# One place in the issue order for every step of a graph-network kernel

## The chip, the cores and the metric

The kernel runs on one core of a Trainium2 chip. It has four compute engines with a queue of their own each: TensorE (PE in the profile, with its weight loads as PEld), VectorE (DVE), ScalarE (ACT) and GpSimd (POOL). SyncE (SP) issues most transfers. Each queue is worked off in the order in which the program issued into it, and an instruction waits by semaphore for what other engines or transfers make. The metric is device time in microseconds, the median of several runs.

## The reference

128 graphs of 64 nodes with 128 features. For every pair of nodes (i, j) of a graph a small network computes a message, the messages of the neighbours are summed, and a second network updates the node:

```python
pair_feats = concatenate([f_i, f_j])               # (128, 64, 64, 256)
messages = _mlp(pair_feats, msg weights) * coupling_matrix[..., None]
agg = sum(messages, axis=2)
updated = part_feats + _mlp(concatenate([part_feats, agg]), upd weights)

def _mlp(x, ...):
    h = layernorm(relu(x @ w0 + b0), g0, be0)
    h = layernorm(relu(h @ w1 + b1), g1, be1)
    return h @ w2 + b2
```

The adjacency is sparse (about one pair in eight, with the diagonal), so the kernel computes messages for existing edges only.

## The kernel before

Each graph gets a list of 640 edge slots, in five tiles of 128. Two graphs are a pair `p` (64 pairs), two pairs a group `q` of 20 tiles (32 groups), four pairs a block `b` (16 blocks). The edge work is done in chunks `n` of four tiles, 512 edges; there are 160 chunks, five to a group.

**Finding the edges, by pair.** `rank`, `count`, `place` and `place_out` number a block's edges. `distance` (ScalarE, L876) and `make_tp` (VectorE, L882) make a 0/1 table of which node owns each slot. `marks` (TensorE, L908) and `compare` (VectorE, L916) make the same for the other node of each edge. `node_rows` and `stack` (transfers on SyncE, L898) lay both tables into the tile `s`. `node_marks` (a transposing transfer, L1018) makes the table for the sums.

**Layer 0, by chunk.** `rows` multiplies the node features by the two halves of w0; `rows_hi` and `rows_lo` split the product into two parts, `abh` and `abl`. `gather` (L933) multiplies them by `s` into the single PSUM bank `hps`, which gives the layer's sums for 512 edges at once. A chunk spans one, two or more stretches of tables that belong to different graphs; each such piece takes two matmuls, for `abl` and `abh`. `relu0` (ScalarE, L938) empties the bank into `h`. `turn_h` (L943) transposes `h` into the single bank `hT`, and VectorE takes `stats0` of it (L629). After a group's five chunks `root_of` makes the standard deviations on ScalarE.

**Layer 1, by chunk.** `layer1` (L986) runs into one of two banks `z`. The bias enters either by `seed` (ScalarE writes it into the bank ahead) or by `seed_all` on GpSimd (L973) with the ReLU on VectorE (L613). `relu1` and `stats1` follow. After a group, `var1_step` (L646, L647, GpSimd; VectorE for the last group), `root1_of` (L653, ScalarE) and `inverse_of` (L658, VectorE) make the factor of the second normalisation. `weights` (L1029, GpSimd) puts it on the table of `node_marks`, and `reduce_block` (L1044) sums the messages of a block's nodes on TensorE.

**Update, by block.** `sums_out`, `turn`, `turn_out`, `layer_a`, `layer_b`, `layer_c`, `layer_out`, `layer_stats`, `upd_*`, `residual`, `bias0` and `finish` run the second network and write the block out.

**The order.** Nothing is scheduled by the framework. The kernel makes a list `plan` of 4,676 steps, each a call of one of these functions, sorts it and calls them one after the other. A step's key is 144 times a chunk number plus an offset from the table `WHEN`. From chunk 14 to 137 the table has one offset for each remainder of the chunk number by ten, so the order repeats every ten chunks (one block); the start and the end have offsets of their own:

```python
def at(n, tag, fn, *args):
    v = args[0] if args else 0
    v = v.b if isinstance(v, Unit) else v
    t = WHEN.get(f"{fn.__name__}{tag}", {}).get(n % 10 if 14 <= n < 138 else 100 + v, 0)
    plan.append((SCALE * n + t, len(plan), fn, args))
```

At the start `keep_busy` (L1336) issues matmuls whose result nobody reads; 18 instructions in seven steps.

Of the kernel before, what the change touches and what calls it, by code (L numbers as in the profile page):

```python
# [25 lines left out]
    "<lambda>.3": {100: 398},  # L26
    "<lambda>.4": {100: 795},
    "<lambda>.6": {100: 4632},
    "<lambda>.7": {100: 284},
    "ahead.0": {100: 233},  # L30
    "ahead.1": {100: 132},
    "ahead.10": {100: 11},
    "ahead.11": {100: -1},
    "ahead.2": {100: 50},
    "ahead.5": {100: 113},
    "ahead.8": {100: 157},
    "ahead.9": {100: 215},
    "bias0": {3: -1471, 112: -1906, 113: -1642, 114: -17},
    "bias0_0": {115: 1153},
    "bias0_2": {115: 525},  # L40
    "bounds": {100: -15375},
# [8 lines left out]
    "count": {8: -190, 101: 140, 102: 122, 115: -186},  # L50
    "count.0": {100: 47},
    "count_out": {9: -228, 101: -2, 102: 190, 115: -239},
    "count_out.0": {100: 63},
    "degrees": {9: -358, 101: -137, 102: 105, 115: -608},
    "degrees.0": {100: -699},
    "distance": {0: -539, 3: 150, 5: -495, 8: -349, 103: 84, 104: 283, 105: -140, 106: 202,
        107: -511, 108: 189, 158: -852, 159: -528, 160: -749, 161: -525, 162: -737, 163: -1005},
    "distance.0": {100: 181},
    "distance.1": {101: 189},
    "distance.2": {102: 311},  # L60
    "empties.0": {100: 111},
    "empties.1": {100: 152},
    "empties.10": {100: 200},
    "empties.11": {100: 169},
    "empties.2": {100: -14},
    "empties.3": {100: 100},
    "empties.4": {100: 111},
    "empties.5": {100: 55},
    "empties.6": {100: -50},
    "empties.7": {100: -92},  # L70
    "empties.8": {100: -22},
    "empties.9": {100: 128},
    "finish": {8: 220, 110: 217, 111: 771, 112: 335, 113: -14, 114: 4865},
    "finish_0": {115: 6154},
    "finish_2": {115: 6519},
    "flag_in": {100: 118},
    "flag_max": {100: 160},
    "flag_out": {100: 377},
    "flag_sum": {100: 514},
    "flag_turn": {100: 45},  # L80
# [26 lines left out]
    "inverse_of": {0: -228, 5: 130, 125: -359, 126: -111, 127: 59, 128: 506, 129: 147, 130: 64,  # L107
# [44 lines left out]
    "layer_out.uh": {7: -98, 112: 370, 113: 251, 114: 103},  # L152
    "layer_out.uy": {2: 270, 111: -27, 112: 407, 113: 290, 114: 1108},
# [222 lines left out]
def tile_gnn(  # L376
# [293 lines left out]
    def edge_path(es):  # L670
# [257 lines left out]
        def gather(n, j, k):  # L928

            if n not in HP:  # L930
                HP[n] = ps_h.tile([P, CH * P], F32, name="hps")
# [727 lines left out]
```

## Time and profile before

| | us |
|---|---|
| median of 3 runs | 498.48 |
| lowest and highest run | 497.48, 499.75 |
| span of the profiled execution | 497.9 |
| TensorE busy (share of the span) | 486.0 (98%) |
| VectorE busy | 465.2 (93%) |
| ScalarE busy | 397.3 (80%) |
| GpSimd busy | 348.4 (70%) |

The span runs from the first to the last instruction of the profiled execution; for that execution no other time is given. A busy time counts stretches in which at least one instruction of the engine is under way. Matmuls overlap and their ends are modelled, so a busy TensorE need not be one at its peak. In a group's row, the numbers after the bar are the busy time in us, the mean duration of one in ns, the idle time of the engine just before them in us, and what ended most of it.

### The profile page before, as it was taken

The numbers are of one execution on the slowest core, as the hardware profiler recorded it, in microseconds if no ns is written. First come the engines' busy times: TensorE is split into PE (matmuls) and PEld (weight loads), VectorE is DVE, ScalarE is ACT, GpSimd is POOL, SyncE is SP. The second block draws the span as 40 slices with busy tenths as digits, with TensorE's granted clock in tenths as the row PEclk, the third lists the DMA queues.
The fourth block names the chain that finished last, engine by engine and source line by source line (L and its number), as shares of the span: only waits on it lengthen the run. The fifth ranks groups of instructions, "written<-read, shape, count | busy, mean of one in ns | idle before, by whom it ended". The sixth has DMA issues, their size and how long they took to land. (4 is left out here: it accounts for less than half of the span.)

```text
span 497.9 us, 15949 instructions
## 1 busy us (share of the span) xinstructions
PE 486.0 (98%) x5947; PEld 461.3 (93%) x5947; DVE 465.2 (93%) x1225; ACT 397.3 (80%) x907; POOL 348.4 (70%) x563
## 2 busy tenths in 40 slices
PE   7999999999999999999999999999999999999995
PEld 5889999999999999999899999999999999999994
DVE  7999999999999999999999999999999988989985
ACT  6999978878787887878778786888878778867754
POOL 3285776967959676795867859676696859565770
PEclk9999999999999999999999999999999999999998
DMA  4766836367574656854465574656655448625331
GB/s 122 148 145 157 182 99 150 93 167 152 126 140 110 126 142 150 168 122 118 117 143 143 126 153 103 132 128 158 152 123 128 101 112 165 152 74 129 66 34 47
DMA packets 91474, 63.55 MB, mean 128 GB/s; under 512 B 57473, under 2 KB 75522, under 8 KB 91394
## 3 DMA queue, kind: packets, MB, share of 16 engines
q1 hardware_dynamic: 91106, 62.36, 55.9%
q8 instruction: 49, 0.80, 0.7%
q14 instruction: 31, 0.25, 0.2%
q10 hardware_dynamic: 288, 0.13, 0.1%
HBM read 7.15 MB, written 4.19 MB: 23 GB/s over the span
## 5 line engine op out<-in xcount | busy, mean ns | idle before, releaser
L986 PE MATMUL z<-w1c,h 128*128 128x128 f32 x1280 | 190.0, 275 | 0.0
L986 PEld LDWEIGHTS z<-w1c,h 128*128 128x128 f32 x1280 | 172.4, 192 | 4.0 <-DVE uy_st L629 0.2
L938 ACT ACTIVATE h<-hps,b0c 128x512 f32<-128x512 f32 x160 | 109.0, 682 | 36.0 <-PE hps L933 35.5
L629 DVE BATCH_NORM_STATS2 st<-hT 128x6 f32<-128x256 f32 x320 | 122.9, 417 | 7.1 <-PE hT L943 4.8
L629 DVE BATCH_NORM_STATS2 st<-y 128x6 f32<-128x256 f32 x320 | 127.1, 419 | 0.5 <-ACT y L997 0.3
L980 ACT ACTIVATE z<-b1b,m_sd 128x128 f32<-128x128 f32 x320 | 117.3, 368 | 9.2 <-DVE y L613 3.6
L943 PE MATMUL hT<-ident,h 128*128 128x128 f32 x640 | 112.9, 276 | 0.3 <-DVE st L629 0.2
L933 PE MATMUL hps<-s,abl 128*128 128x512 f32 (+3 forms) x256 | 96.6, 380 | 2.6 <-ACT h L938 2.1
L933 PE MATMUL hps<-s,abh 128*128 128x512 f32 (+3 forms) x256 | 89.8, 358 | 0.0
L973 POOL TENSOR_TENSOR u<-b1b,m_sd 128x512 f32<-128x512 f32 x80 | 83.7, 1049 | 7.6 <-ACT m_sd L637 7.6
L943 PEld LDWEIGHTS hT<-ident,h 128*128 128x128 f32 x640 | 76.3, 141 | 3.4 <-issue 1.2
L1029 POOL TENSOR_TENSOR w<-oh,m_q 128x192 f32<-128x192 f16 x126 | 62.1, 514 | 9.4 <-DVE m_q L658 3.1
L916 DVE TENSOR_TENSOR j<-mk,cmpt 128x320 fp32r<-128x320 f32 x124 | 59.4, 479 | 6.3 <-PE mk L908 3.9
L891 POOL CAST i<-tp 128x640 fp32r<-128x640 f16 x58 | 41.8, 720 | 29.3 <-DMA s<-i 27.7
L997 ACT ACTIVATE y<-z 128x512 f32<-128x512 f32 x80 | 47.4, 595 | 17.8 <-PE z L986 17.5
L613 DVE CUSTOM_DVE_ANT_0 y<-z,u 128x512 f32<-128x512 f32 x80 | 54.1, 676 | 4.0 <-PE z L986 3.7
L933 PEld LDWEIGHTS hps<-s,abl 128*128 128x128 f32 x256 | 48.8, 191 | 8.0 <-ACT h L938 3.7
L876 ACT ACTIVATE d<-slot,mid 128x640 f16<-128x640 f16 x64 | 52.1, 818 | 1.7 <-POOL mid L765 1.0
L647 POOL TENSOR_TENSOR m_v<-m_v,st 128x20 f32<-128x20 f32 x31 | 7.3, 234 | 60.9 <-DVE st L629 59.6
L933 PEld LDWEIGHTS hps<-s,abh 128*128 128x128 f32 x256 | 49.1, 192 | 0.2
L1044 PE MATMUL ys<-y,w 128*32 128x128 f32 x1488 | 44.1, 274 | 0.0
L1044 PEld LDWEIGHTS ys<-y,w 128*32 128x32 f32 x1488 | 39.6, 110 | 2.5 <-issue 2.1
(193 smaller groups left out, 887.9 us busy)
## 6 DMA issues: line engine op xcount, KB each, us to landing
s<-i SPq DMA_DIRECT2D x124, 160.0 KB, 3.0
s<-j SPq DMA_DIRECT2D x124, 160.0 KB, 2.8
xn<-in_x_dram SPq DMA_DIRECT2D x15, 256.0 KB, 3.9
out_dram<-uo SPq DMA_DIRECT2D x15, 256.0 KB, 2.5
an<-in_adj_dram SPq DMA_DIRECT2D x16, 128.0 KB, 3.5
oh<-tp SPq DMA_TRANSPOSE x64, 3.0
xn<-in_x_dram SPq DMA_DIRECT2D x2, 128.0 KB, 3.0
out_dram<-uo SPq DMA_DIRECT2D x2, 128.0 KB, 3.4
```

What stands on the lines that cost most here:

```text
L613: nc.vector._custom_dve(TENSOR_ADD_SAT, out=o, in0=ps, in1=sb, s0=BIG, s1=0.0)
L629: nc.vector.bn_stats(st, src.rearrange("p t c -> p c t"))
L876: nc.scalar.activation(D[p], slot.rearrange("p (t e) -> p t e", e=P), AF.Abs, bias=blocks[b]["mid"][:, q:q + 1], scale=-1.0)
L916: nc.vector.tensor_tensor(JR[p][:, c], MK.pop((p, k))[:, 0:HC], cmpt[:, c], op=ALU.is_equal)
L933: nc.tensor.matmul(HP[n][:, c:c + w], lhsT=blocks[g // (2 * PB)]["ab", g // 4 % 2][k][:, g % 4, :], rhs=S[g // 2][:, g % 2, e:e + w], star ...
L938: nc.scalar.activation(H[n], HP.pop(n), AF.Relu, bias=b0c)
L943: nc.tensor.transpose(HT[n][:, t, :], H[n][:, t * P:(t + 1) * P], ident)
L973: nc.gpsimd.tensor_tensor(U[n], bc(W["b1b"], CH), SR[q][:, k:k + CH].unsqueeze(2).to_broadcast([P, CH, C]), op=ALU.mult)
L980: nc.scalar.activation(z_of(n)[:, t, :], W["b1b"], AF.Copy, scale=SR[q][:, k:k + 1])
L986: nc.tensor.matmul(ps[:, t, :], lhsT=H[n][:, t * P:(t + 1) * P], rhs=W["w1c"], start=by_vector(n) and t == 0, stop=True, skip_group_check= ...
L1029: (nc.vector if p == NP - 2 else nc.gpsimd).tensor_tensor(WT[p][:, g], oh, qs, op=ALU.mult)
L1044: nc.tensor.matmul(YS[b][g * N + m * HN:g * N + (m + 1) * HN, k, :], lhsT=w[:, g, m, u, :], rhs=y, start=(u == 0), stop=(u == TH - 1), til ...
```

## The change

The table holds, for every kind of step, one place for each time that the step is put on the list, from 1 to 4,676, each used once. The key is that place alone; chunk number and period no longer enter. Four functions change beside it. `gather` counts the matmuls that a chunk still has to get: the first to be issued, whichever piece it is, has `start`, the last has `stop`, and the others accumulate; before, each piece had a `start` and a `stop` of its own. `upd_shift`, `marks_here` and `rows_here` make their tile in whichever of their steps comes first.

```diff
 WHEN = {
-    "keep_busy.n2": {102: -390},
-    "root1_of": {0: -276, 5: 96, 125: -363, 126: -204, 127: -15, 128: 436, 129: 138, 130: 40,
-        131: 200},
...
+    "keep_busy.n2": (11,),
+    "root1_of": (
+        464, 572, 738, 834, 963, 1131, 1228, 1415, 1533, 1657, 1781, 1955, 2169, 2300, 2439, 2570,
+        2699, 2854, 2989, 3101, 3319, 3396, 3575, 3695, 3842, 3925, 4136, 4259, 4398, 4474, 4557,
+        4603),
...
+        seen = {}
+
         def at(n, tag, fn, *args):
-            v = args[0] if args else 0
-            v = v.b if isinstance(v, Unit) else v
-            t = WHEN.get(f"{fn.__name__}{tag}", {}).get(n % 10 if 14 <= n < 138 else 100 + v, 0)
-            plan.append((SCALE * n + t, len(plan), fn, args))
+            base = f"{fn.__name__}{tag}"
+            k = seen[base] = seen.get(base, -1) + 1
+            t = WHEN[base][k] if base in WHEN else SCALE * n
+            plan.append((t, len(plan), fn, args))
...
         def gather(n, j, k):
-            if n not in HP:
+            start = n not in HP
+            if start:
                 HP[n] = ps_h.tile([P, CH * P], F32, name="hps")
+                LEFT[n] = 2 * len(list(pieces(n)))
+            LEFT[n] -= 1
             g, e, c, w = sorted(pieces(n), key=lambda v: -v[3])[j]
             nc.tensor.matmul(HP[n][:, c:c + w], lhsT=blocks[g // (2 * PB)]["ab", g // 4 % 2][k][:, g % 4, :],
-                             rhs=S[g // 2][:, g % 2, e:e + w], start=(k == 0), stop=(k == 1))
+                             rhs=S[g // 2][:, g % 2, e:e + w], start=start, stop=LEFT[n] == 0,
+                             skip_group_check=True)
...
         def upd_shift(u, q0, q1):
-            if q0 == 0:
-                u.usdb = wide("usdb", u)
+            u.usdb = wide("usdb", u)
...
         def marks_here(p):
-            S[p] = sp.tile([P, 2, CAP], F32R, name="s")
+            if p not in S:
+                S[p] = sp.tile([P, 2, CAP], F32R, name="s")
...
         def rows_here(p, g):
+            if p not in S:
+                S[p] = sp.tile([P, 2, CAP], F32R, name="s")
             nc.scalar.copy(S[p][0:N, g, :], TP[p][g * N:(g + 1) * N])
```

Some places before and after, counted in the sorted list of 4,676 steps:

| step | place before | place after |
|---|---|---|
| `turn_x`, first block, first half | 11 | 1 |
| the three first `keep_busy` | 4, 5, 6 | 11, 24, 26 |
| `relu0` of chunk 0 | 46 | 41 |
| `layer1` of chunk 0 | 168 | 158 |
| last `reduce` | 4,617 | 4,618 |

More of the change, by code (lines that the diff above doesn't have):

```diff
@@ L25 @@
 WHEN = {
[L26 to L41, printed above, removed]
[8 rows of a table removed]
@@ L50 @@
[L50 to L80, printed above, removed]
[26 rows of a table removed]
-    "inverse_of": {0: -228, 5: 130, 125: -359, 126: -111, 127: 59, 128: 506, 129: 147, 130: 64,
[44 rows of a table removed]
-    "layer_out.uh": {7: -98, 112: 370, 113: 251, 114: 103},
-    "layer_out.uy": {2: 270, 111: -27, 112: 407, 113: 290, 114: 1108},
[12 rows of a table removed]
-    "load_adj": {1: -693, 102: -349, 103: -1531},
-    "load_x": {8: -290, 102: 631, 115: 184},
-    "make_tp": {1: -374, 4: 131, 6: -444, 9: -342, 103: 108, 104: 179, 105: 120, 106: 96, 107: -74,
[10 rows of a table removed]
@@ L179 @@
-    "node_marks": {0: -545, 4: 10, 5: 367, 9: -143, 100: -798, 101: 174, 152: 17, 153: 333,
-        154: 534, 155: -146, 156: 563, 157: 63, 158: 368, 159: 445, 160: 688, 161: 506, 162: -255,
-        163: -43},
-    "node_rows": {0: -314, 2: 91, 5: 223, 7: -155, 102: 278, 103: 417, 104: 90, 105: 101, 106: 65,
-        107: -131, 158: -226, 159: 2, 160: -311, 161: 40, 162: 463, 163: 314},
-    "odd_weights": {3: -24, 101: -1531, 102: -1295, 115: -539},
-    "odd_weights.0": {100: -1392},
-    "ones": {100: 12389},
@@ L187 @@
-    "place": {1: -331, 101: 214, 102: -38, 115: -472},
-    "place_first": {100: 127},
-    "place_out": {3: 174, 101: 237, 102: -124, 115: -233},
-    "place_pair.0": {100: 184},
-    "place_rest": {100: 187},
-    "rank": {6: -208, 101: 117, 102: -33},
-    "rank.0": {100: -830},
-    "reduce.-1": {163: 277},
-    "reduce.-2": {162: 257},
-    "reduce.-3": {161: 385},
-    "reduce.-4": {160: 269},
-    "reduce.-5": {159: -276},
-    "reduce.-6": {158: -297},
-    "reduce.-7": {157: 717},
-    "reduce.-8": {156: 598},
@@ L370 @@
-    "weights.1.1": {2: -269, 7: -112, 151: -490, 153: 294, 155: 117, 157: 234, 159: 279, 161: 259,
-        163: 359},
+    "<lambda>.3": (1060,),
+    "<lambda>.4": (304,),
+    "<lambda>.6": (1214,),
+    "<lambda>.7": (449,),
+    "ahead.0": (57,),
+    "ahead.1": (83,),
+    "ahead.10": (118,),
+    "ahead.11": (148,),
+    "ahead.2": (94,),
+    "ahead.5": (112,),
+    "ahead.8": (108,),
+    "ahead.9": (121,),
+    "bias0": (
+        4434, 4179, 3829, 3691, 3196, 2996, 2673, 2175, 1912, 1614, 1212, 1335, 1106, 910, 523),
@@ new lines @@
+    "bias0_0": (4487,),
+    "bias0_2": (4334,),
+    "bounds": (1174,),
[14 rows of a table added]
+    "count": (19, 203, 442, 654, 1014, 1286, 1598, 1860, 2130, 2444, 2738, 3027, 3336, 3556, 3894),
+    "count.0": (4,),
+    "count_out": (
+        28, 218, 472, 679, 1029, 1308, 1599, 1867, 2167, 2459, 2762, 3033, 3346, 3568, 3910),
+    "count_out.0": (6,),
+    "degrees": (39, 200, 517, 646, 956, 1241, 1503, 1744, 2023, 2075, 2643, 3049, 3317, 3479, 3787),
+    "degrees.0": (9,),
+    "distance": (
[19 rows of a table added]
+    "finish": (
+        4659, 4595, 4512, 4295, 3993, 3702, 3395, 3093, 2836, 2542, 2262, 1949, 1660, 1396, 1054),
@@ new lines @@
+    "finish_0": (4673,),
+    "finish_2": (4676,),
+    "flag_in": (4180,),
+    "flag_max": (4347,),
+    "flag_out": (4524,),
+    "flag_sum": (4523,),
+    "flag_turn": (4333,),
[48 rows of a table added]
+    "inverse_of": (
[64 rows of a table added]
+    "layer_out.uh": (
+        4612, 4430, 4200, 3919, 3605, 3328, 3031, 2713, 2469, 2145, 1892, 1548, 1309, 990, 716),
+    "layer_out.uy": (
+        4633, 4551, 4326, 4072, 3727, 3474, 3154, 2913, 2594, 2292, 1977, 1727, 1429, 1144, 819),
+    "layer_out_0.uh": (4625,),
+    "layer_out_0.uy": (4650,),
@@ new lines @@
+    "layer_out_2.uh": (4643,),
+    "layer_out_2.uy": (4663,),
+    "layer_stats.uh.0": (
+        4613, 4440, 4216, 3965, 3625, 3347, 3062, 2758, 2522, 2158, 1897, 1549, 1317, 1016, 729),
+    "layer_stats.uh.2": (
+        4619, 4483, 4289, 3980, 3689, 3417, 3071, 2861, 2523, 2161, 1918, 1622, 1366, 1019, 730),
+    "layer_stats.uy.0": (
+        4634, 4552, 4336, 4079, 3755, 3484, 3157, 2919, 2617, 2342, 2025, 1758, 1457, 1164, 848),
+    "layer_stats.uy.2": (
+        4639, 4566, 4374, 4144, 3769, 3533, 3185, 2920, 2649, 2355, 2081, 1761, 1469, 1199, 889),
@@ new lines @@
+    "layer_stats_0.uh.0": (4629,),
+    "layer_stats_0.uy.0": (4651,),
+    "layer_stats_2.uh.0": (4646,),
+    "layer_stats_2.uy.0": (4666,),
+    "load_adj": (150, 282, 435, 420, 671, 1278, 1543, 1624, 1830, 2360, 2365, 2680, 3014, 3320),
+    "load_x": (194, 399, 559, 1038, 1379, 1413, 1718, 2177, 2220, 2487, 2811, 3235, 3531, 4006),
+    "make_tp": (
[19 rows of a table added]
+    "node_marks": (
[5 rows of a table added]
+    "node_rows": (
[4 rows of a table added]
+    "odd_weights": (
+        89, 227, 620, 866, 1025, 1436, 1721, 1816, 2324, 2600, 2889, 3211, 3777, 4100, 4160),
@@ new lines @@
+    "odd_weights.0": (5,),
+    "ones": (2446,),
+    "place": (63, 236, 558, 827, 1057, 1353, 1638, 1933, 2223, 2465, 2868, 3141, 3414, 3594, 3972),
+    "place_first": (7,),
+    "place_out": (
+        127, 279, 613, 897, 1180, 1394, 1707, 1938, 2304, 2488, 2869, 3179, 3448, 3612, 4034),
+    "place_pair.0": (10,),
+    "place_rest": (30,),
+    "rank": (14, 176, 314, 622, 862, 1203, 1456, 1692, 1976, 2008, 2568, 2910, 3222, 3418, 3725),
+    "rank.0": (3,),
+    "reduce.-1": (4618,),
+    "reduce.-2": (4617,),
@@ new lines @@
+    "reduce.-3": (4598,),
+    "reduce.-4": (4593,),
+    "reduce.-5": (4563,),
+    "reduce.-6": (4562,),
+    "reduce.-7": (4530,),
+    "reduce.-8": (4515,),
+    "reduce_block": (
[28 rows of a table added]
+    "residual": (
+        4616, 4538, 4373, 3786, 3759, 3056, 3202, 2691, 2325, 1708, 2115, 1547, 1086, 633, 665),
+    "residual_0": (4597,),
+    "residual_2": (4526,),
+    "root1_of": (
+        464, 572, 738, 834, 963, 1131, 1228, 1415, 1533, 1657, 1781, 1955, 2169, 2300, 2439, 2570,
+        2699, 2854, 2989, 3101, 3319, 3396, 3575, 3695, 3842, 3925, 4136, 4259, 4398, 4474, 4557,
+        4603),
@@ new lines @@
+    "root_of": (
+        157, 271, 412, 532, 681, 807, 962, 1100, 1257, 1392, 1532, 1682, 1846, 1980, 2114, 2245,
+        2417, 2549, 2693, 2824, 2964, 3134, 3284, 3402, 3577, 3723, 3858, 3977, 4125, 4255, 4406,
+        4521),
+    "rows.0": (88,),
+    "rows.0.0.0.2": (12,),
+    "rows.0.0.2.4": (15,),
+    "rows.1": (34, 303),
+    "rows_both": (339, 609, 832, 1190, 1446, 1760, 2055, 2328, 2620, 2917, 3175, 3487, 3747, 4143),
[44 rows of a table added]
+    "seed_all": (
[76 rows of a table added]
+    "sums_out": (
[73 rows of a table added]
+    "turn_out.uh": (
+        4627, 4511, 4307, 3974, 3665, 3386, 3096, 2828, 2499, 2219, 1957, 1670, 1400, 1089, 733),
@@ new lines @@
+    "turn_out.uy": (
+        4647, 4570, 4444, 4112, 3879, 3549, 3291, 2990, 2709, 2440, 2104, 1843, 1595, 1281, 997),
+    "turn_out.ysum": (
+        4594, 4329, 4078, 3854, 3543, 3275, 2962, 2682, 2389, 2063, 1815, 1510, 1215, 939, 649),
+    "turn_out_0.uh": (4637,),
+    "turn_out_0.uy": (4668,),
+    "turn_out_0.ysum": (4615,),
+    "turn_out_2.uh": (4655,),
+    "turn_out_2.uy": (4669,),
+    "turn_out_2.ysum": (4635,),
+    "turn_x": (51, 248, 499, 785, 1110, 1410, 1702, 1974, 2229, 2531, 2838, 3104, 3403, 3675, 4119),
@@ new lines @@
+    "turn_x.0": (16,),
+    "turn_x.0.0.2": (1,),
+    "turn_x_out": (
+        66, 317, 569, 814, 1123, 1419, 1703, 1983, 2241, 2585, 2852, 3105, 3466, 3737, 4121),
+    "turn_x_out.0.0.2": (2,),
+    "turn_x_out_rest": (18,),
+    "upd_inverse": (
+        4656, 4586, 4449, 4266, 3989, 3681, 3387, 3018, 2788, 2533, 2239, 1931, 1587, 1314, 1048),
+    "upd_inverse_0": (4672,),
+    "upd_inverse_2": (4675,),
+    "upd_m1": (
+        4641, 4578, 4376, 4191, 3778, 3604, 3205, 2966, 2725, 2460, 2131, 1765, 1479, 1265, 978),
@@ new lines @@
+    "upd_m1_0": (4652,),
+    "upd_m1_2": (4667,),
+    "upd_root0": (
+        4620, 4500, 4291, 4019, 3712, 3446, 3084, 2897, 2553, 2189, 1961, 1643, 1387, 1046, 772),
+    "upd_root0_0": (4638,),
+    "upd_root0_2": (4660,),
+    "upd_root1": (
+        4648, 4579, 4415, 4219, 3789, 3635, 3263, 3013, 2753, 2468, 2147, 1817, 1496, 1297, 1037),
+    "upd_root1_0": (4662,),
+    "upd_root1_2": (4670,),
+    "upd_shift": (4321, 4020, 3716, 3459, 3095, 2899, 2590, 2207, 1966, 1711, 1403, 1083, 788),
@@ new lines @@
+    "upd_shift.0": (4631, 4545),
+    "upd_shift.2": (4632, 4543),
+    "upd_shift_0.0": (4640,),
+    "upd_shift_2.0": (4661,),
+    "var1_step": (
+        415, 557, 731, 793, 948, 1091, 1225, 1373, 1522, 1645, 1756, 1944, 2153, 2297, 2436, 2566,
+        2698, 2829, 2982, 3100, 3282, 3383, 3566, 3694, 3831, 3923, 4122, 4256, 4384, 4461, 4556,
+        4602),
+    "weights.0.0": (
+        553, 580, 799, 872, 1109, 1146, 1374, 1435, 1551, 1737, 1871, 1987, 2269, 2313, 2480, 2611,
+        2808, 2870, 3048, 3145, 3322, 3431, 3640, 3706, 3933, 3982, 4215, 4297, 4475, 4520, 4574,
+        4606),
@@ new lines @@
+    "weights.0.1": (
+        489, 579, 782, 871, 1042, 1136, 1381, 1444, 1666, 1738, 1861, 1999, 2186, 2307, 2495, 2601,
+        2750, 2876, 3029, 3155, 3335, 3430, 3643, 3730, 3900, 3975, 4271, 4298, 4503, 4504, 4580,
+        4609),
+    "weights.1.0": (
+        525, 581, 797, 849, 1045, 1142, 1267, 1417, 1559, 1724, 1865, 1992, 2287, 2320, 2504, 2608,
+        2853, 2885, 3117, 3140, 3326, 3458, 3636, 3711, 3889, 3998, 4254, 4281, 4472, 4498, 4583,
+        4607),
+    "weights.1.1": (
+        493, 599, 826, 860, 1070, 1155, 1322, 1427, 1574, 1740, 1834, 1972, 2302, 2317, 2567, 2584,
+        2826, 2880, 3065, 3151, 3401, 3472, 3660, 3744, 3958, 3976, 4247, 4288, 4410, 4493, 4577,
+        4605),
```

55 lines of the change are left out of this document (1 added, 54 removed), and 605 rows, old and new, of the table WHEN.

## Prediction

> **What bounds the kernel now.** I read the page first, then the busy time by stretches, then the waits, then the order of time around the longest wait. The page's span, its TensorE row, the granted clock and two groups:
>
> ```profile
> span 497.9 us, 15949 instructions
> PE 486.0 (98%) x5947; PEld 461.3 (93%) x5947; DVE 465.2 (93%) x1225; ACT 397.3 (80%) x907; POOL 348.4 (70%) x563
> PEclk9999999999999999999999999999999999999998
> L986 PE MATMUL z<-w1c,h 128*128 128x128 f32 x1280 | 190.0, 275 | 0.0
> L938 ACT ACTIVATE h<-hps,b0c 128x512 f32<-128x512 f32 x160 | 109.0, 682 | 36.0 <-PE hps L933 35.5
> ```
>
> TensorE is busy in 98% of the span. The stretches (time, busy time of PE, PEld, DVE, ACT and POOL, granted clock, DMA) say where its idle time lies:
>
> ```profile
> core 0: us, PE busy (x) PEld busy (x) DVE busy (x) ACT busy (x) POOL busy (x), PEclk, DMA share, GB/s
> 25.00:475.00 450.00, 447.21 (x5537) 429.32 (x5538) 429.01 (x1123) 366.39 (x834) 332.95 (x526) 1.00 0.59 132
> 1.90:6.50 4.60, 4.59 (x13) 3.58 (x14) 2.64 (x8) 2.55 (x6) 2.11 (x5) 1.00 0.85 213
> 6.50:13.00 6.50, 5.51 (x52) 3.34 (x51) 6.34 (x14) 6.10 (x13) 0.91 (x2) 1.00 0.34 86
> 13.00:25.00 12.00, 11.56 (x136) 9.81 (x135) 11.18 (x32) 11.65 (x27) 3.26 (x7) 1.00 0.77 154
> 475.00:492.00 17.00, 16.94 (x224) 15.27 (x216) 13.76 (x43) 10.08 (x30) 7.93 (x16) 1.00 0.07 18
> ```
>
> From 25 to 475 us TensorE is idle for 450.00 - 447.21 = 2.79 us. From 6.5 to 25 us it is idle for 0.99 + 0.44 = 1.43 us, and there VectorE and ScalarE are nearly full too. From 475 to 492 us it is idle for 0.06 us. Six us more are the end, where the last output is written. So an order of issue that adds and removes no work can win little in sight. A modelled matmul end hides a little more, since a wait shows only after that end:
>
> ```profile
> 201.94 1.06 PE L986 MATMUL z<-w1c,h 128*128 128x128 f32 x8
> ```
>
> Eight matmuls take 1.06 us and one takes 0.275, so the next starts (1.06 - 0.275) / 7 = 0.112 us later. A wait is thus 0.275 - 0.112 = 0.16 us longer than the idle time shown. What TensorE waited for (total, times, longest), and two waits of other engines:
>
> ```profile
> PE hps L933 <- ACT h L938: 2.1, 5, 0.6
> PE ys L1336 <- DVE first L521: 1.9, 1, 1.9
> PE ma L819 <- DMA xn<-in_x_dram: 0.4, 1, 0.4
> ...
> POOL m_v L647 <- DVE st L629: 59.6, 18, 5.1
> ACT m_sq L653 <- POOL m_v L647: 10.2, 12, 1.6
> ```
>
> Five waits make 2.1 of the 2.79 us: the gather of the next chunk waits until ScalarE's ReLU (L938) has emptied the one bank `hps`. Here is the longest of them, first ScalarE's queue, then TensorE:
>
> ```profile
> 244.82 0.69 ACT L938 ACTIVATE h<-hps,b0c 128x512 f32<-128x512 f32 x1
> 247.07 0.31 ACT L653 ACTIVATE m_sq<-m_v,eps_c 128x20 f32<-128x20 f32 x1 [1.56 <-POOL m_v L647]
> 247.28 0.57 ACT L856 CAST abh<-mu 128x512 fp32r<-128x512 f32 x1
> 247.75 0.60 ACT L997 ACTIVATE y<-z 128x512 f32<-128x512 f32 x1
> 248.24 0.69 ACT L938 ACTIVATE h<-hps,b0c 128x512 f32<-128x512 f32 x1
> ...
> 246.62 0.40 PE L933 MATMUL hps<-s,abh 128*128 128x512 f32 x1
> ...
> 248.98 0.44 PE L933 MATMUL hps<-s,abl 128*128 128x384 f32 x1 [0.64 <-ACT h L938]
> ```
>
> `root1_of` (L653) stands at the head of ScalarE's queue for 1.56 us, because `var1_step` on GpSimd has not written `m_v`. Behind it stand a copy, a ReLU and then the ReLU of the gather, which ended at 246.62 + 0.40 = 247.02 and is read only at 248.24. The gather starts 0.05 us after that ReLU's end.
>
> **The change part by part.** No engine gains or loses an instruction: the same 4,676 steps are issued in another order. I sorted the steps by the old table and by the new one and compared places. Half of them move by 14 places or more; 29 places are one chunk, about 3 us, so a place is near 498 / 4,676 = 0.106 us.
>
> *Gather flags.* One `start` for the chunk's first piece and one `stop` for its last, with the same matmuls: 0. The moved tile allocations in `upd_shift`, `marks_here` and `rows_here` issue nothing: 0.
>
> *`root1_of` behind `var1_step`.* Over groups 2 to 27 the old order puts the root three places or fewer behind `var1_step` 13 times, which goes with the 12 ScalarE waits above; the new order does so 8 times. The five waits that reached TensorE cost 2.1 + 5 x 0.16 = 2.9 us. They belong to groups 8, 16, 18, 20 and 24; there the distance goes from 3 to 11, 1, 7, 37 and 11. I count four of five as gone: -0.8 x 2.9 = **-2.3 us**, with 0 and -2.9 as ends. The stall that goes from ScalarE is late next only at `inverse_of` on VectorE and `weights` on GpSimd, which stand some 41 places (4.4 us) later than they did; the sums over nodes that read the weights move by 15. GpSimd is idle for 450 - 333 = 117 us of the middle and covers it.
>
> *Covers that get shorter.* Laying the matmuls out at the distances of the rows, I compared the work between two steps of TensorE. Between the last gather of a chunk and the first of the next the smallest is 0.38 us before and 0.88 after, the median 1.49 and 1.48. What has to fit is the row of L938, 0.69, plus 0.05, plus the 0.2 by which the ReLU lies behind the start of the following matmul (0.04 behind the modelled end, as below): 0.94. So nine places of the new order are short, by 0.18 us together: 0.
>
> ```profile
> 11.20 0.39 PE L933 MATMUL hps<-s,abh 128*128 128x512 f32 x1
> 11.63 0.69 ACT L938 ACTIVATE h<-hps,b0c 128x512 f32<-128x512 f32 x1 [0.35 <-PE hps L933]
> ```
>
> From that last gather to the chunk's own transposes the smallest goes from 1.48 to 0.78 and the median from 2.51 to 2.15; from the transposes to those of the next chunk, whose bank `hT` VectorE must empty, from 1.08 to 0.56 and from 1.97 to 1.49. These are thinner and I can't see from one order alone when VectorE and ScalarE reach their part. I take 0; the upper end is the slower rival below.
>
> *Transfers.* `load_adj` and `load_x` move by 203 and 95 places on average, `node_marks` by 122, the `stack` copies by 43, all on SyncE's queue. For each I took the latest step that it or anything ahead of it in that queue waits for, and counted to its first reader. For `stack` the least is 32 places before and 30 after, some 3.2 us, and the median rises from 90 to 105; for `load_x` the least is 74 (7.8 us), for `node_marks` 18 (1.9 us). To landing they take:
>
> ```profile
> s<-i SPq DMA_DIRECT2D x124, 160.0 KB, 3.0
> xn<-in_x_dram SPq DMA_DIRECT2D x15, 256.0 KB, 3.9
> oh<-tp SPq DMA_TRANSPOSE x64, 3.0
> ```
>
> So one `weights` on GpSimd may wait 1.1 us, under the same idle time as above: 0. `residual` (222 places) and `bias0` (159) move within GpSimd's queue: 0, and up to 1.3 us at one point if a seed for VectorE's ReLU stands behind.
>
> *The start.* Before, six dummy matmuls (`keep_busy`) run first, while TensorE has nothing to do; now `turn_x` is first and they come 11, 24 and 26 steps in, others up to place 110.
>
> ```profile
> 1.91 2.93 PE L1336 MATMUL ys<-first,mean_m 128*128 128x256 f32 x6 [1.91 <-DVE first L521]
> 4.70 0.67 PE L819 MATMUL hT<-ident,xn 128*128 128x128 f32 x2
> ...
> 8.47 1.56 PE L1336 MATMUL ys<-first,mean_m 128*128 128x256 f32 x6
> ```
>
> The same six take 2.93 us at first and 1.56 at 8.47, so TensorE is slow at first and becomes fast after some us of work. In the new order its first work is that of 4.70 us, 2.8 us later. Against that, the first layer-1 step stands behind less VectorE work: `rank`, `odd_weights` and a `compare` for later blocks move behind it, two `make_tp` ahead, about 0.7 + 0.9 + 0.5 - 2 x 0.54 = 1.0 us less, on an engine that is 6.34 of 6.50 us busy there. I take **-0.5 us**, with -1.0 and +2.9 as ends; the latter is all real matmul work ahead of the first ReLU, 2.9 us at the fast rate, run at half of it. [...]
>
> *The end* keeps its order but for neighbours that swap, and TensorE is idle 0.06 us there: 0, plus or minus 0.5.
>
> **Sum:** -2.3 - 0.5 = -2.8. The profiled span, 497.9, becomes 495.1. It lies 0.6 under the median of the runs, 498.48, and inside their 497.48 to 499.75; 498.48 - 2.8 = **495.7 us**.
>
> **The rivals.** *The wait moves (same).* Eight close pairs remain, five of them in odd groups, which had the root 19 places behind before. If these block ScalarE for 1.3 to 1.6 us as the twelve did, and two in five reach TensorE as five in twelve did, three waits of 0.6 come back, 1.7 us: 498.48 - 2.8 + 1.7 = 497.4. For it: `root1_of` in group 16 stands two places behind the group's last statistics. Against it: in the other close pairs `var1_step` itself stands later.
>
> *A cold start (same).* TensorE stays slow while the first chunks need it: 498.48 - 2.3 + 2.9 = 499.1. For it: the two durations of the dummies. Against it: until 13 us VectorE sets the pace.
>
> *The transposes wait (slower).* The new order sets a chunk's transposes a median of 0.36 us of matmuls nearer to the ReLU that makes their input. ScalarE had to wait for TensorE in only 54 of 160 such ReLUs, so in the others it came late:
>
> ```profile
> ACT h L938 <- PE hps L933: 35.5, 54, 1.8
> ```
>
> If the whole 0.36 is missing in one chunk, TensorE loses it. From about 15 of 160 chunks on (5.4 us) this outweighs the gain of 2.8 and the bound of 2.5; with 18 it is 6.5 us: 498.48 - 2.8 + 6.5 = 502.2. For it: the least distance, 0.78, is under the 0.94 needed. Against it: at a tenth of the chunks the distance still leaves 0.39 us over the need (1.03 before).
>
> **How the numbers follow.** Forecast 0.58, the wait moves 0.18, cold start 0.08, the transposes wait 0.16. A measurement of this kernel tells about 0.5% (2.5 us) from no change. The forecast's own range is 492 to 498: all idle time of the middle and half of the start's gone gives 498.48 - 2.9 - 0.7 - 0.7 = 494.2, and waits under 0.16 us, which no row shows, may add two more. Four fifths of it I count as faster, with a little from the wait that moves: 0.49; same 0.33; slower 0.18. The range for 8 in 10 is 491.5 to 501.5.
>
> **What would show it.** Idle time of TensorE from 25 to 475 us near 0.5 to 1 us; at most two waits of `hps` for `h`; ScalarE's wait for `m_v` clearly under 10.2 us; the first dummies later than 4.7 us and the first gather within 0.5 us of 10.86. The forecast is wrong if `hT` waits for `h` or `st` for more than 3 us, or if TensorE's busy time itself grows or shrinks by more than 3 us, since the same 5,947 matmuls are issued.

## The result, and the profile after

| | before | after |
|---|---|---|
| median of 4 runs, us | 498.24 | 580.66 |
| lowest and highest run, us | 497.48, 499.75 | 579.01, 581.69 |
| span of the profiled execution, us | 497.9 | 577.2 |

The ratio is 1.166 (95% interval 1.162 to 1.169): the new order is 82 us slower. The prediction said 495.7 us, with 501.5 as its upper end. It was wrong in sign and by a size that none of its cases held.

The page of the kernel after: the span, the engines, and groups of instructions with their busy time, the mean of one in ns, and the idle time ahead of them with what ended it.

```profile
span 577.2 us, 15855 instructions
PE 517.6 (90%) x5947; PEld 463.4 (80%) x5947; DVE 475.7 (82%) x1225; ACT 400.0 (69%) x907; POOL 350.2 (61%) x563
L837 DVE BATCH_NORM_STATS2 st<-hT 128x6 f32<-128x256 f32 x320 | 129.6, 421 | 54.1 <-PE hT L1157 52.2
L1157 PE MATMUL hT<-ident,h 128*128 128x128 f32 x640 | 132.2, 282 | 41.7 <-DVE st L837 40.1
L1152 ACT ACTIVATE h<-hps,b0c 128x512 f32<-128x512 f32 x160 | 109.4, 684 | 79.2 <-PE hps L1146 78.0
L1200 PE MATMUL z<-w1c,h 128*128 128x128 f32 x1280 | 182.0, 277 | 4.3 <-ACT z L1194 3.9
```

The lines moved: the statistics `two_stats` are L837 (L629 before), `turn_h` L1157 (L943), `relu0` L1152 (L938), `gather` L1146 (L933), `layer1` L1200 (L986), `seed` L1194 (L980).

The instructions still take what they took (421 ns for a statistics step, 684 ns for a ReLU). What is new is that they wait for each other. The same two groups of the kernel before:

```profile
L629 DVE BATCH_NORM_STATS2 st<-hT 128x6 f32<-128x256 f32 x320 | 122.9, 417 | 7.1 <-PE hT L943 4.8
L943 PE MATMUL hT<-ident,h 128*128 128x128 f32 x640 | 112.9, 276 | 0.3 <-DVE st L629 0.2
```

VectorE now waits 52.2 us for transpositions (4.8 before), and the transpositions wait 40.1 us for VectorE's statistics (0.2 before). Two engines that wait for each other over one tile point at the bank `hT`. One chunk (number 34) in the order of time shows it; a row is the start, the duration, the instruction, and in brackets the idle time of its engine and who ended it.

```profile
118.86 0.49 PE L1157 MATMUL hT<-ident,h 128*128 128x128 f32 x3
...
119.39 0.43 DVE L837 BATCH_NORM_STATS2 st<-hT 128x6 f32<-128x256 f32 x1 [0.47 <-PE hT L1157]
...
119.87 0.33 PE L1157 MATMUL hT<-ident,h 128*128 128x128 f32 x1 [0.53 <-DVE st L837]
...
120.24 0.43 DVE L837 BATCH_NORM_STATS2 st<-hT 128x6 f32<-128x256 f32 x1 [0.42 <-PE hT L1157]
```

A chunk's four transpositions write the four parts of `hT`. The first statistics step reads parts 0 and 1, the second parts 2 and 3. Here three transpositions run. Then VectorE reads parts 0 and 1 from 119.39 to 119.82, and the fourth transposition, which writes part 3 and so touches nothing of what is read, starts only at 119.87, 0.05 us after that reader's end. TensorE stands still for 0.53 us, and behind it in its queue everything else does too.

The places in the list of 4,676 steps say why:

| chunk 34 | `turn_h` 0, 1, 2, 3 | `stats0` 0, 2 |
|---|---|---|
| before | 939, 942, 943, 946 | 947, 950 |
| after | 935, 936, 937, 945 | 940, 946 |

In the new order the first `stats0` stands between the third and the fourth transposition. Counted over the two sorted lists, that is so in **78 of 160 chunks** (39 times one transposition stands behind the statistics step, 39 times two), and in none of the old list. In TensorE's queue other work stands between the two transpositions in 52 of the 78 chunks. From the start of the matmul just ahead, whatever it is, to the start of the first transposition behind the reader it takes 0.8 us in the median of the 78. Together these steps take 61 us of the trace, where transpositions that follow each other would take 78 x 0.11 = 9.

The start changed as well. TensorE's first rows after:

```profile
4.10 0.66 PE L1029 MATMUL hT<-ident,xn 128*128 128x128 f32 x2 [4.10 <-DMA xn<-in_x_dram]
...
7.34 0.43 PE L1044 MATMUL mu<-w0a,xnT 128*32 128x128 f32 x2 [0.49 <-ACT abh L1066]
...
9.74 0.47 PE L1118 MATMUL z<-tp,posall 128*128 128x320 f16 x1
...
11.50 0.30 PE L1044 MATMUL ma<-w0a,xnT 128*32 128x128 f32 x2
...
12.51 0.50 PE L1146 MATMUL hps<-s,abl 128*128 128x512 f32 x1
```

TensorE's first work comes at 4.10 us in place of 1.91, since `turn_x` heads its queue and waits for a transfer. At 7.34 us two matmuls of `rows` still take 0.43 us, at 11.50 us 0.30, and at 9.74 one of `marks` takes 0.47. The same work in the kernel before, with its first gather:

```profile
7.67 0.30 PE L908 MATMUL z<-tp,posall 128*128 128x320 f16 x1
7.90 0.30 PE L834 MATMUL mu<-w0a,xnT 128*32 128x128 f32 x2
10.86 0.50 PE L933 MATMUL hps<-s,abl 128*128 128x512 f32 x1 [0.34 <-DVE abl L867]
```

The first gather starts at 12.51 us, 1.65 us later than before, and the first layer-1 matmul at 29.41 us, 4.9 us later than the 24.51 of before.

### The profile page after: what moved, and what is told of

It is laid out like the page before. It is cut to its first block, busy times and chain, and to the rows that moved or that the text cites. A ratio compares the mean times of both kernels' runs of the same rounds, so it can differ in the third digit from the quotient of the medians.

```text
span 577.2 us, 15855 instructions
## 1 busy us (share of the span) xinstructions
PE 517.6 (90%) x5947; PEld 463.4 (80%) x5947; DVE 475.7 (82%) x1225; ACT 400.0 (69%) x907; POOL 350.2 (61%) x563
## 4 chain that ended last, share of the span: by engine, by line
## 5 line engine op out<-in xcount | busy, mean ns | idle before, releaser
L1200 PE MATMUL z<-w1c,h 128*128 128x128 f32 x1280 | 182.0, 277 | 4.3 <-ACT z L1194 3.9
L837 DVE BATCH_NORM_STATS2 st<-hT 128x6 f32<-128x256 f32 x320 | 129.6, 421 | 54.1 <-PE hT L1157 52.2
L1200 PEld LDWEIGHTS z<-w1c,h 128*128 128x128 f32 x1280 | 164.3, 192 | 11.7 <-ACT z L1194 8.3
L1157 PE MATMUL hT<-ident,h 128*128 128x128 f32 x640 | 132.2, 282 | 41.7 <-DVE st L837 40.1
L1152 ACT ACTIVATE h<-hps,b0c 128x512 f32<-128x512 f32 x160 | 109.4, 684 | 79.2 <-PE hps L1146 78.0
L1157 PEld LDWEIGHTS hT<-ident,h 128*128 128x128 f32 x640 | 78.4, 141 | 68.5 <-DVE st L837 56.1
L1194 ACT ACTIVATE z<-b1b,m_sd 128x128 f32<-128x128 f32 x320 | 117.0, 369 | 23.4 <-PE z L1200 11.6
L837 DVE BATCH_NORM_STATS2 st<-y 128x6 f32<-128x256 f32 x320 | 126.6, 418 | 1.5 <-ACT y L1211 0.8
L1146 PE MATMUL hps<-s,abl 128*128 128x384 f32 (+3 forms) x256 | 94.2, 385 | 0.3 <-ACT h L1152 0.3
L1243 POOL TENSOR_TENSOR w<-oh,m_q 128x192 f32<-128x192 f16 x126 | 63.7, 526 | 41.9 <-DVE m_q L866 28.1
L1146 PE MATMUL hps<-s,abh 128*128 128x128 f32 (+3 forms) x256 | 84.7, 349 | 0.0
L1086 ACT ACTIVATE d<-slot,mid 128x640 f16<-128x640 f16 x64 | 52.2, 823 | 4.6 <-DVE tp L1092 3.9
L1146 PEld LDWEIGHTS hps<-s,abl 128*128 128x128 f32 x256 | 47.7, 192 | 4.0 <-issue 2.2
L1146 PEld LDWEIGHTS hps<-s,abh 128*128 128x128 f32 x256 | 48.2, 193 | 0.1
```

The source lines that it names most:

```text
L837: nc.vector.bn_stats(st, src.rearrange("p t c -> p c t"))
L1086: nc.scalar.activation(D[p], slot.rearrange("p (t e) -> p t e", e=P), AF.Abs, bias=blocks[b]["mid"][:, q:q + 1], scale=-1.0)
L1146: nc.tensor.matmul(HP[n][:, c:c + w], lhsT=blocks[g // (2 * PB)]["ab", g // 4 % 2][k][:, g % 4, :], rhs=S[g // 2][:, g % 2, e:e + w], star ...
L1152: nc.scalar.activation(H[n], HP.pop(n), AF.Relu, bias=b0c)
L1157: nc.tensor.transpose(HT[n][:, t, :], H[n][:, t * P:(t + 1) * P], ident)
L1194: nc.scalar.activation(z_of(n)[:, t, :], W["b1b"], AF.Copy, scale=SR[q][:, k:k + 1])
```

## Experiments

Each kernel ran on a chip on which the kernel before ran too, with medians of 498.3 to 498.6 us. The notation of the edits: `at_place[function, arguments]` is a step's place in the list ahead of its sorting. The edits are shown by the lines that matter; loops over chunks and the lines that collect the places and put them back are left out.

**The split, undone (first theory).** The theory: a write into the bank waits for each earlier-issued reader of that bank, whatever part it reads, so a statistics step between two transpositions stalls the second. The rival was the seeds of `layer1`: in 17 chunks a seed stands behind the first matmuls of its bank.

```diff
+for n in range(NCHK):
+    turned = max(at_place["turn_h", (n, t)] for t in range(CH))
+    at_place["stats0", (n, 0)] = max(at_place["stats0", (n, 0)], turned + 0.5)
```

> The changed kernel with one thing undone: the first statistics step of a chunk (stats0 of tiles 0 and 1) is put behind the chunk's last transposition, in the 78 chunks where the new places put it ahead of one. Theory A (a transposition waits for any reader of its bank hT, also of another part of it): in the trace of the changed kernel the next transposition starts 0.055 us after that statistics step's end in nearly all 78 chunks, and these steps take 61 us where 78 x 0.11 = 9 would do; so at least 52 of the 82 us come back and the time is 500 to 528. Theory B (ScalarE's ReLU or VectorE's queue is late because all covers are thinner, and the split only marks where it shows): less than 20 us come back, the time stays above 560, and the wait of hT goes to other instructions.

Measured: 537.33 us, ratio 1.078 [1.075, 1.081]; 43.3 us less than the change. Its span and two of TensorE's longest waits, then two of the other engines' (total, times, longest):

```profile
span 536.0 us, 15904 instructions
PE z L1200 <- ACT z L1194: 6.1, 12, 1.2
PE hT L1157 <- DVE st L837: 4.2, 13, 0.5
...
ACT h L1152 <- PE hps L1146: 53.1, 71, 2.3
DVE st L837 <- PE hT L1157: 36.7, 56, 1.6
```

The transpositions' wait falls from 40.1 us to 4.2, and the time by somewhat more. That is less than the 52 us that the theory asked for and more than the 20 of its rival. The split carries half of the loss, and the other half isn't explained by it.

**The seeds, moved ahead.** The 23 seeds go ahead of `layer1`'s first matmuls:

```diff
+if ("seed", (n, t)) in at_place:
+    at_place["seed", (n, t)] = min(at_place["seed", (n, t)],
+                                   at_place["layer1", (n, 0)] - 0.5)
```

> The changed kernel with another thing undone: in the 17 chunks where 23 seeds (ScalarE writing the bias into the bank z) stand behind the chunk's first layer-1 matmuls, they are put ahead of them. Theory A, same mechanism in another bank: the trace of the changed kernel shows 3.9 us of TensorE waiting for a seed and 11.6 us of ScalarE waiting for TensorE before one, so 3 to 8 us come back: 573 to 578. Theory B: no change, 580.

Measured: 582.08 us in one run, no gain. With both edits:

> Both of the foregoing in one kernel. Theory A: 495 to 520; if what is left of the new places is as good as was forecast, 495.7. Theory B: above 555.

Measured: 540.35 us, 1.084 [1.081, 1.086], no better than the first edit alone. The rival falls: moving these seeds won nothing, although they stand between two writes to a bank as the statistics step does.

**The split alone, put into the old order.** In the same 78 chunks the first `stats0` is issued between the second and the third transposition; nothing else of the old table moves.

```diff
+for n in split:                                   # the 78 chunks
+    at_place["stats0", (n, 0)] = max(at_place["turn_h", (n, t)] for t in range(2)) + 0.5
+    for t in range(2, CH):
+        at_place["turn_h", (n, t)] = max(at_place["turn_h", (n, t)],
+                                         at_place["stats0", (n, 0)] + 0.25)
```

> The kernel before, with its table, but in the same 78 chunks the first statistics step is issued between the second and the third transposition. Theory A: each costs 0.2 + 0.42 + 0.055 us less the work of TensorE in between, 0.5 to 0.9 us: 498 + 78 x 0.7 = 553, between 535 and 570, and the next transposition starts 0.055 us after the statistics' end. Theory B: VectorE takes half of a chunk's statistics earlier and nothing waits: 496 to 502.

Measured: 567.67 us, 1.139 [1.136, 1.141]. That is 69.2 us for 78 chunks, 0.89 us each. The groups show the picture of the change:

```profile
L629 DVE BATCH_NORM_STATS2 st<-hT 128x6 f32<-128x256 f32 x320 | 129.1, 420 | 71.9 <-PE hT L943 70.2
L943 PE MATMUL hT<-ident,h 128*128 128x128 f32 x640 | 127.5, 283 | 52.0 <-DVE st L629 51.5
```

So this pattern alone makes the old kernel 14% slower. It is a cause, shown in both directions.

**The other way round, and by halves.** Instead of delaying the statistics step, the late transpositions are pulled ahead of it:

```diff
+read = at_place["stats0", (n, 0)]
+for t in range(2, CH):
+    at_place["turn_h", (n, t)] = min(at_place["turn_h", (n, t)], read - 0.75 + t / 8)
```

> The changed kernel with the split undone from the other side: the late transpositions are pulled ahead of the chunk's first statistics step, which keeps its place on VectorE. Theory A (the split is what costs): as good as moving the statistics, 537, or better, 515 to 535, since the statistics no longer move later and the next chunk's transpositions wait less for them (11.5 us over 41 such waits were left there). Theory B2 (what was left there comes from VectorE's own order being late): 535 to 545.

Measured: 535.55 us, 1.074 [1.069, 1.079], so 45.1 us less than the change, as good as moving the statistics step. And the first edit in every second of the 78 chunks only:

> The changed kernel with the statistics moved behind the last transposition in 39 of the 78 chunks, every second one. Theory A with a fixed price for each split: half of the 43.3 us that all 78 gave, 559 plus or minus 4. If a few large ones make the loss, or if the waits only move on to the next chunk, it lies outside 550 to 568.

Measured: 561.75 us, 1.126 [1.122, 1.130]: 18.9 us less, near half of 43.3. The loss goes by the number of splits.

**The flags alone.** The old order with the new `start` and `stop` of `gather`:

```diff
-    rhs=..., start=(k == 0), stop=(k == 1))
+    rhs=..., start=start, stop=LEFT[n] == 0, skip_group_check=True)
```

> The kernel before, its table kept, with the new start and stop flags of the gather alone (one start for a chunk's first piece, one stop for its last). Both theories: no instruction is added, 496 to 501. If the flags had a part in the 82 us, this is slower than 505.

Measured: 498.12 us, 1.000 [0.998, 1.002]: nothing, as predicted.

**The start.** With the transpositions ahead of the statistics, the first 230 steps of the old order are put ahead of all others, in their old sequence:

```diff
+plan = [(early_order[i] - 1e5, i, f, a) if i in early_order else (t, i, f, a)
+        for t, i, f, a in plan]
```

> As the kernel with the transpositions pulled ahead, and its first 230 steps in the order of the table before (until layer 1 of chunk 2), with the six dummy matmuls first. The traces show the first layer-1 matmul 4.9 us later in the changed kernel and TensorE at half speed until about 10 us in place of 6.5. Theory A' (the start is a loss of its own): 4 to 6 us less than the kernel with the transpositions ahead. If the start's lateness is made up later under the slack of the other engines: 0 to 1 us less.

Measured: 531.50 us, 1.066 [1.062, 1.070]; 4.05 us less than with the new start. Its first layer-1 matmul comes at 24.53 us, as in the kernel before; in the run without the old start it comes at 28.17. So the start is a loss of its own, as the cold-start rival said, with 4.05 in place of its 2.9 us. The run moves the whole start, so it doesn't tell the slow matmuls from the other order of the work. It leaves 33 us. Its span and five of its waits:

```profile
span 530.0 us, 15895 instructions
ACT h L1152 <- PE hps L1146: 52.0, 67, 2.4
DVE st L837 <- PE hT L1157: 33.4, 56, 1.6
PEld z L1200 <- ACT z L1194: 12.4, 26, 1.3
PE z L1200 <- ACT z L1194: 6.2, 12, 1.1
PE hT L1157 <- DVE st L837: 2.2, 7, 0.5
```

**What is left, tried one wait at a time.** First `layer1`'s first matmuls behind the last seed of their chunk:

```diff
+seeded = max(at_place["seed", (n, t)] for t in range(CH))
+at_place["layer1", (n, 0)] = max(at_place["layer1", (n, 0)], seeded + 0.25)
```

> The kernel with the old start and the transpositions ahead of the statistics (531.5), and in the 17 chunks where seeds stand behind the chunk's first layer-1 matmuls these matmuls are moved behind the last seed. There are 10.3 us of TensorE waiting for a seed at 22 places; six of them (3.4 us) follow a seed that itself waited for layer-1 matmuls in the same bank. If the shared bank is the cause, 3 to 5 us come back: 527 to 529. If ScalarE is late for other reasons: 530 to 533.

Measured: 533.08 us, 1.070 [1.068, 1.072], no gain. Then, on top of it, a chunk's transpositions at least 11 places behind those of the chunk before, so that VectorE has time to empty `hT`:

```diff
+free = max(at_place["turn_h", (n - 1, t)] for t in range(CH)) + 11
+for t in range(CH):
+    at_place["turn_h", (n, t)] = max(at_place["turn_h", (n, t)], free + t / 8)
```

> As the foregoing, and the transpositions of a chunk stand at least 11 places (1.2 us) behind the last transposition of the chunk before. 8 us of TensorE waiting for the statistics were left at 33 places, nearly all behind a VectorE that had just waited for the same bank's transpositions: bank hT goes round too fast. If that is so, 4 to 8 us come back against the foregoing. If VectorE is late through its own queue, the wait stays and 0 to 2 us come back.

Measured: 533.32 us, 1.071 [1.068, 1.073], no gain either.

**Short covers alone, in the old order.** A cover is the work that TensorE has between two steps, while another engine does its part. The prediction's slower rival held that transpositions too near to the ReLU that feeds them make TensorE wait. Here the first two transpositions of a chunk are issued earlier in the old order, without a split. By the layout of TensorE's queue that the prediction used, the work between the last gather and the transpositions falls from a median of 2.51 us to 2.09 (new order: 2.15), and that between the transpositions of two chunks from 1.97 to 1.66 (new order: 1.49).

```diff
+free = max(at_place["relu0", (n,)], at_place["stats0", (n - 1, 2)] + 10)
+for t in range(2):
+    at_place["turn_h", (n, t)] = min(at_place["turn_h", (n, t)],
+        max(at_place["turn_h", (n, t)] - 20, free + 0.5 + t / 8))
```

> The kernel before; only the first two transpositions of a chunk are issued earlier, so that the work of TensorE between a chunk's gather and its transpositions falls from a median of 2.51 us to 2.09 (smallest 1.48 to 1.17), and between the transpositions of two chunks from 1.97 to 1.66 (smallest 1.08 to 0.48), close to the new order (2.15 and 0.78, 1.49 and 0.56). No statistics step is split off. The prediction's slower rival (thin covers make the transpositions wait): 502 or more. If covers this thin don't cost by themselves: 497 to 500.

Measured: 512.74 us, 1.029 [1.027, 1.031], 14.4 us slower. The waits:

```profile
ACT h L938 <- PE hps L933: 51.5, 69, 1.9
DVE st L629 <- PE hT L943: 16.2, 39, 1.0
PE hT L943 <- DVE st L629: 7.5, 14, 1.3
```

Under half a microsecond of cover is worth 14 us by itself, and ScalarE's wait for gathers rises to 51.5 us (35.5 before), as in the split-free new order (52.0). But the wait is not the one that the rival named. The longest, in chunk 103:

```profile
312.10 0.69 ACT L938 ACTIVATE h<-hps,b0c 128x512 f32<-128x512 f32 x1 [0.99 <-PE hps L933]
...
314.20 0.41 DVE L629 BATCH_NORM_STATS2 st<-hT 128x6 f32<-128x256 f32 x1
...
314.76 0.41 PE L943 MATMUL hT<-ident,h 128*128 128x128 f32 x2 [1.30 <-DVE st L629]
```

The ReLU that makes `h` ended at 312.79, 2 us earlier. The transposition starts 0.15 us after the step that reads the last of chunk 102 out of `hT`. Counted from 25 us on, the first transposition of 56 chunks starts so, 0.15 us after that step's end (7 in the kernel before), and in one chunk its weights are loaded right behind the ReLU's end. By an estimate from the trace, which sets each step from one matmul's start to the next against the median of its kind in the kernel before, the 56 lose 13.9 us (the 7 of before 1.2). So the short cover that costs is the one between the transpositions of two chunks, in which VectorE must empty `hT`.

**Longer covers, in the new order.** Three runs on the kernel that took 531.50 us. The gathers and their ReLU are issued up to 10 places earlier, which lays 2.82 us of TensorE's work between gather and transposition:

```diff
+at_place["gather", (n, j, k)] = min(t, max(t - 10, made + 0.25 + k / 16 + j / 8))
...
+at_place["relu0", (n,)] = min(t, max(t - 10, last + 0.5))
```

`made` is the place of the last step that makes the gather's operands, or two places behind `relu0` of the chunk before; `last` is the chunk's last gather.

> The new order with the transpositions ahead of the statistics and the old start (531.5 us) is taken as it is, and from chunk 8 on the gather and the ReLU behind it are issued up to 10 places earlier (9 on average, about 1 us). Laid out, the work of TensorE between the last gather of a chunk and its first transposition rises from a median of 2.12 us to 2.82 (the old order has 2.51). If the shorter cover here carries most of the 33 us that are left, 10 to 20 us go: 512 to 522. If the 33 us are many small collisions of other kinds, the time stays within 3 us of 531.5, and the waits of VectorE for the transpositions stay near 33 us.

Measured: 591.96 us, 1.188 [1.185, 1.192], 60 us slower, where 10 to 20 us less or nothing was expected. The waits say where it went:

```profile
ACT h L1152 <- PE hps L1146: 77.3, 74, 4.8
DVE st L837 <- PE hT L1157: 64.0, 76, 6.2
...
PE hps L1146 <- ACT h L1152: 23.7, 38, 3.7
```

The gathers now arrive before ScalarE has emptied the one bank `hps`: they wait 23.7 us for the ReLU of the chunk before. In the change that wait was 0.3 us, and in the kernel before 2.1. The cover behind the gather was bought with the one ahead of it, so the run can't say what a longer cover is worth.

Then the seeds up to 12 places earlier, and both edits together:

```diff
+free = max(at_place["relu1", (n - 2,)], at_place["root_of", (n // QC,)]) + 0.5
+at_place["seed", (n, t)] = min(p, max(p - 12, free + t / 8))
```

> From the same kernel (531.5 us), 304 of 320 seeds are issued up to 12 places earlier (9 on average, about 1 us), behind the ReLU that empties their bank. There the weight loads of layer 1 wait 12.4 us in 26 places for a seed of ScalarE. If these waits come from where the seeds stand, 6 to 12 us go: 519 to 525. If ScalarE as a whole is late because it waits for gathers (52 us), the seeds stay late: within 3 us of 531.5, and the waits for seeds stay above 8 us.

Measured: 539.67 us, 1.083 [1.081, 1.084], 8 us slower, where 6 to 12 us less or nothing was expected. Two waits:

```profile
PEld z L1200 <- ACT z L1194: 8.4, 14, 1.3
...
PE hps L1146 <- ACT h L1152: 4.7, 8, 1.1
```

The weight loads of `layer1` wait 8.4 us for seeds in place of 12.4, which is the lesser gain hoped for. But the seeds take ScalarE's time ahead of the ReLUs, and the gathers wait 4.7 us for those.

> Gathers, their ReLUs and the seeds are all issued earlier, as in the two kernels beside it. If both covers count and are independent, the gains add up. If one lateness of ScalarE is behind both, the gain is that of the better one. If neither counts, 528 to 535.

Measured: 591.10 us, 1.186 [1.183, 1.189], the time of the earlier gathers alone.

**The one part that was forecast to win, alone.** In the old order only the `root1_of` of every second group moves, from close behind `var1_step` to 30 further on in the old table's keys:

```diff
-    "root1_of": {0: -276, 5: 96, ...
+    "root1_of": {0: -276, 5: 126, ...
```

> The kernel before; in even groups root1_of stands 30 keys later, behind the ReLU of the next chunk (relu0), so that a late var1_step no longer holds up that ReLU. The prediction's first term (five waits of TensorE, 2.9 us): 495.6 to 496.6. If the gain is lost elsewhere, at the reciprocal and the weights: 497.5 to 499.

Measured: 496.97 us, 0.9966 [0.9944, 0.9987], 1.35 us faster. Three waits:

```profile
PE hps L933 <- ACT h L938: 0.2, 1, 0.2
PE hT L943 <- DVE st L629: 0.2, 1, 0.2
ACT y L997 <- PE z L986: 25.3, 46, 1.4
```

That is just above the 495.6 to 496.6 that was expected. The gathers' wait for the ReLU falls from 2.1 us in five places to 0.2 in one, as the prediction described it. ScalarE's wait at L997 rises from 17.5 to 25.3 us beside it. This is the only version that beats both kernels, by less than the 0.5% that a measurement of this kernel tells from no change.

## Why the prediction was wrong

**The step that failed is "Covers that get shorter", taken at 0.** It measured distances from the last gather to the transpositions and from the transpositions of one chunk to those of the next. It treated a chunk's four transpositions as one block with the reader behind it. In the new order they are no block: in 78 chunks the reader of parts 0 and 1 stands among them. The same sorted lists that gave the distances had this in them. One more count, the readers that stand between two writes to the same tile, would have shown 78 against 0. Undoing the split gave 43 and 45 us, undoing half of it 19, and adding it to the old order cost 69. Counting by the parts that are read and written would have missed them: in chunk 34 the fourth transposition starts 0.05 us after the end of a reader of other columns.

**The mutual wait is a chain in one queue.** The price is not the 0.43 us of the reader alone. The reader is late first: in the chunk shown it starts 0.04 us after the third transposition's end, though it reads only parts 0 and 1, and VectorE idles for 0.47 us. Then comes the reading, and then 0.05 us. With one transposition's own step of 0.11 us taken off, 0.8 us of step leave about 0.7 us per split; alone in the old order a split cost 0.89 us. In the change the gain from undoing it was 43.3 / 78 = 0.56 us each. There other work of TensorE stands between in 52 chunks and covers part of the wait; by the estimate of the run with short covers, the transpositions behind such a reader lose 47.8 us from 25 us on, 0.6 each. And with the split undone by the first edit, what is lost behind `hT` of the chunk before grows from 6.9 us to 13.0.

**The slower rival had the direction, not the mechanism.** "The transposes wait" expected them to wait for the ReLU that makes `h`, and 502.2 us. They waited for `st` instead: in the change mostly behind the split, and with short covers alone behind `hT` of the chunk before, in 56 chunks against one for the ReLU. So those 14.4 us are no support for the rival, although they are more than twice its 6.5. They belong to the other distance that "Covers that get shorter" measured and took at 0, the one from the transpositions to those of the next chunk. Distances alone take VectorE as always on time. In chunk 103 two other statistics steps stood in its queue between the two of chunk 102 (at 313.53 and 313.86 us), and the bank came free late.

**The other terms.** "`root1_of` behind `var1_step`" (-2.3 us): right in mechanism, since TensorE's wait is 0.2 us once in the run that moves it alone and 0.3 us once in the change, and ScalarE's wait for `m_v` falls from 10.2 us to 1.9 in the change. The size isn't settled: moved alone, for all five waits (2.9 us), it gave -1.35 us, with -2.8 to -0.6 by the interval's ends. "Gather flags" (0): measured 0. "The start" (-0.5, bounds -1.0 and +2.9): +4.05 us, outside its bounds. The dummies that come later were weighed, but the lesser work on VectorE was taken to outweigh them; the first gather came 1.65 us later, not within 0.5 us of 10.86. TensorE's work began later and its matmuls were slow until later, but the time since the first work alone doesn't say until when: at 9.74 us, 5.6 us after the first work and behind two idle gaps of about 0.5 us, a `marks` matmul still takes 0.47 us, while in the kernel before one takes 0.30 at 7.67 us, 5.8 us after the first work and behind one gap of 0.24. "Transfers" (0) had no run of its own; in the waits after, GpSimd waits 1.4 us for `stack` transfers, less than the 27.7 of before, and TensorE waits for a transfer only at the start. "The end" (0, plus or minus 0.5) had no run either; from the start of the last layer-1 matmul to the end the trace shows 21.0 us after and 20.3 before, 0.7 more.

**What it named as proof against itself came true.** `hT` waits for `st` for 40.1 us (bound 3), and TensorE's busy time grew from 486.0 to 517.6 us with the same 5,947 matmuls.

**The account.** Of 82 us, about 45 are the split and 4 the start. About 33 us are left, nearly all in the middle. Against the trace of the kernel before, the ReLU of chunk 40 comes 6 us later in the run of 531.50 us, that of chunk 80 16 us, of chunk 120 22 and of chunk 159 30.

The trace divides the 33 us further, by the same estimate. At 22 places a matmul of `layer1` starts 0.05 us after the end of a seed in its bank: 10.6 us (0.2 us at one place before). In 44 chunks the first transposition starts 0.15 us after `hT` of the chunk before is read: 9.2 us (1.2 in 7 before). Behind the ReLU there is nothing. The other 14 us or so are shorter delays in many places. The prediction had no term for the first of these: in the sorted lists a seed stood a median of 28 places ahead of its matmuls and 17 at the lowest tenth, and in the new order 21.5 and 7. Distance alone doesn't explain it, since with the seeds earlier (29 and 16) weight loads still waited 8.4 of the 12.4 us.

Moving `layer1`, spacing the transpositions, and issuing gathers or seeds earlier didn't win any of it back; the last two only moved the wait to another single bank or to ScalarE's queue. That a shorter cover at `hT` costs time is shown; why the seeds come late, and what the other delays come from, stays open. Whether a second bank for `hT` would free the transpositions was not tried.

## What to carry to other kernels

When the order of issue changes, list for every PSUM bank the writes and readers in issue order and look for a reader that now stands between two writes; here each such place in `hT` cost 0.9 us, put alone into the old order, though writer and reader touched different parts. The seeds that stood so in `z` cost nothing that a run showed, so a count of such places is a list of suspects and not a price. Only then compare distances, for every pair of a step and the one that frees its bank or makes its input, and compare their low end with how late the other engines really are, not with an instruction's duration. Where `hps` and `hT` are single banks and three engines are 80 to 98% busy, moving one kind of step earlier mostly moved the wait: 10 places for the gathers cost 60 us.

## What the runs showed of the hardware that was not expected

A transposition into one part of `hT` started 0.05 us after the end of a statistics step that read other parts of the same bank, in 71 of the 78 places. The wait is the program's: it shows as a semaphore of VectorE. No run here left it out, so whether the chip needs it is not shown. The second surprise is how far the slow start reaches: the same `rows` matmuls took 0.43 us at 7.34 us after work that began at 4.10, and 0.30 at 7.90 after work that began at 1.91. Only the durations show it; the granted clock of the profile reads 1.00 from 4.1 to 7.3 us too.
